# Even spacing of replicated loads, later GpSimd products and re-paced side DMAs in a selective-scan kernel

## Chip, cores and metric

The kernel runs on one core of a Trainium2 chip. The metric is the device time of one execution in microseconds; the median of several runs is given.

## What is computed

The reference is a network of four layers on four images of 64x64 positions and 96 channels. Nearly all of what follows concerns the selective scan of layer 0, cut here to what matters:

```python
x_hw = xc.reshape(B, D_INNER, L)                  # rows first; D_INNER = 192, L = 4096
x_wh = transpose(xc, (0, 1, 3, 2)).reshape(B, D_INNER, L)   # columns first
xs = concatenate([x_hw, x_wh, flip(x_hw), flip(x_wh)])
# per direction, image, channel d and state s (16 states):
#   h[t] = exp(delta[d, t] * A[d, s]) * h[t-1] + delta[d, t] * u[d, t] * B[s, t]
#   y[d, t] = sum over s of h[t] * C[s, t]
yy = y_rows + y_columns_turned_back + the two reversed ones
x = x + (yy * silu(z)) @ W_out.T
```

After it come, for each image, a depthwise and pointwise convolution (layer 1), a linear attention with a quantised feed-forward (layer 2), and a Fourier filter with another quantised feed-forward (layer 3). All data are float32.

## The kernel before

**Stages.** First the inputs of the scan of image 0 are made (projection, 3x3 convolution, softplus, products). Then comes the scan stage, an order written out by hand, and beside it run two lanes of other work. The drain and `tail()` handle what is left, above all layers 1 to 3 of image 3.

**Scan steps.** A half is one image in one order: `o = 0` is rows, `o = 1` is columns. `halves` (L1296) lists the eight of them. A half has 24 groups of 8 channels, so that 8 channels x 16 states fill 128 partitions; a group is a step, and `phases` lists all 192. A step covers the 4096 positions in four chunks of 1024. The loop at L1511 issues a step in eight slots, named f0 to f3 here (forward, `q` = 0 to 3) and b0 to b3 (backward, `k` = 0 to 3, chunk 3 - `k`).

In slot f`q`, VectorE scans chunk `q` forward from `pa` and `B` into `S` (L1534). In slot b`k` it scans backward into `pa` (L1581), saves the edge (L1587) and adds the two (L1588). Around it:

- ScalarE makes `pa` = exp(delta x A) in PSUM (`decay`, L1351), two buffers, seven times a step, one slot ahead.
- GpSimd multiplies delta·u by B (`times_b`, L1341) and the summed states by C (`times_c`, L1345), in place: `times_b(n + 1, q - 1)` in f1 to f3 and `times_b(n + 1, 3)` in b0 for the next step, `times_c` in b1 to b3 and in the next f0.
- TensorE sums over the states (`reduce`, L1361), ScalarE copies the sum (`result`, L1369), and SyncE stores it in four DMAs for each half of the positions (`store_result`, L1378).
- SyncE loads `dl` (`load_delta`) and `B` (`load_du`), four chunks each a step, every one replicated over 16 states in two DMAs (L1313). Tile `dl` has five buffers, `B` eight, `S` five. `load_rep` (L1336) fetches B and C of a new half into `rep0` and `rep1`, four chunks each.

SyncE issues all DMAs of the kernel in program order. Its DMAs take turns on eight completion semaphores, and a DMA waits until the one eight places before it has landed. Below, dl1 means `load_delta` of chunk 1, du3 `load_du` of chunk 3.

**Side lanes.** After each slot `pieces` (L1427) adds credit to five resources (TensorE, ScalarE, GpSimd, VectorE, DMA) from that slot's row of `gains` (L1419) and lets generators go on as far as their costs fit. The side lane transposes the scan inputs of an image for the columns (`turns`), turns the columns' result back (`turn_back`) and gates and projects it (`post`). These copies run on ScalarE (L166), with stores at L133 and `sz` products on VectorE at L514. A `turn` store takes 1.6 of DMA credit. The main lane first makes the scan inputs of images 1 to 3 (ScalarE `u`, L392; GpSimd, L469 to L477) and then works through layers 1 to 3 of images 0 to 2 (`rest`; feed-forward matmuls L967 and L987, ScalarE rows L958 to L996). `post` of an image waits for `done["scans", b]`, and `turn_back` for `done["columns", b]`. Which side operation falls into which slot is thus decided when the program is built.

Of the kernel before, what the change touches and what calls it, by code (L numbers as in the profile page):

```python
# [18 lines left out]
NB = 4  # L19
# [52 lines left out]
def layers(ctx: ExitStack, tc: tile.TileContext, a: dict, out):  # L72
# [101 lines left out]
    def halves_of(src, dst):  # L174
        return [(src[k * C : (k + 1) * C, :], dst[k * C : (k + 1) * C, :]) for k in range(2)]

    def turns(side, b):

        yield from until(lambda: done.get(("back", b), 0) == NBLK)
        pairs = [(bc_s[0][b], bc_s[1][b])]  # L180
        for s in (delta_s, du_s):
            pairs += halves_of(s[0][b], s[1][b])
        yield from turn(side, pairs)
        done["turns", b] = True

    def turn_back(side, b):

        yield from until(lambda: ("columns", b) in done)
        yield from turn(side, halves_of(y_s[1][b], y2_s[b]))
# [45 lines left out]
    def until(ready):  # L235
        while not ready():
            yield NEXT
# [1021 lines left out]
    def side_lane(take, side):  # L1259


        def place(name, k):
            at = 8 if name == "xr" else 2 * ("y_in", "u_in", "y2_in", "sz_in").index(name) + k % 2
            return side[:, at * BLK : (at + 1) * BLK]

        steps = [turns(side, 0), turns(side, 1), turn_back(side, 0), post(place, take, 0, 1)]
        steps += [turns(side, 2), turns(side, 3), turn_back(side, 1), post(place, take, 1, 1)]
        steps += [turn_back(side, 2), post(place, take, 2, 1), turn_back(side, 3)]
        for s in steps:
            yield [s], []  # L1270
# [22 lines left out]
        return slice(q * CH, (q + 1) * CH)  # L1293


    halves = [(b, o) for b in range(NB) for o in ((0, 1) if b < NB - 1 else (1, 0))]  # L1296
    phases = [(b, g, o) for b, o in halves for g in range(NG)]
    N = len(phases)
    dls, Bs, Ss, reps, pys, yss = {}, {}, {}, {}, {}, {}
# [1 line left out]
    def place_of(n, q):  # L1301


        return (4, 3, 2, 1)[q] if n % 2 else q
# [5 lines left out]
    def load_channels(t, src, g, q):  # L1310
        for k, part in enumerate(channel_halves(t)):
            rows = src[g * 8 + k * 4 : g * 8 + k * 4 + 4, chunk(q)]
            nc.sync.dma_start(part, rows.unsqueeze(0).broadcast_to([NS, 4, CH]))  # L1313

    def load_delta(n, q):
        if n < N:
            b, g, o = phases[n]
            t = dls[n, q] = big.tile([128, CH], F32, tag=f"dl{place_of(n, q)}", name="dl")
            load_channels(t, delta_s[o][b], g, q)
# [18 lines left out]
    def times_b(n, q):  # L1338

        if n < N:  # L1340
            nc.gpsimd.tensor_tensor(Bs[n, q], Bs[n, q], reps[n // NG, 0, q], ALU.mult)  # L1341

    def times_c(n, q):
        if n >= 0:
            nc.gpsimd.tensor_tensor(Ss[n, q], Ss[n, q], reps[n // NG, 1, q], ALU.mult)  # L1345
# [8 lines left out]
    def reduce(n, half):  # L1354

        if n < 0:
            return
        py = pys[n, half] = ps.tile([128, BLK], F32, tag="py", name="py")
        for j in range(4):
            q, k = 2 * half + j // 2, j % 2  # L1360
            nc.tensor.matmul(  # L1361
                py[32 * j : 32 * j + 32, :], lhsT=red, rhs=Ss[n, q][:, k * BLK : (k + 1) * BLK],
                start=True, stop=True,
            )

    def result(n, half):
        if n >= 0:
            ys = yss[n, half] = big.tile([128, BLK], F32, tag="ys", name="ys", bufs=2)
            nc.scalar.copy(ys, pys.pop((n, half)))  # L1369

    def store_result(n, half):
        if n < 0:
            return
        b, g, o = phases[n]
        ys = yss.pop((n, half))
        for j in range(4):
            i = 4 * half + j
            nc.sync.dma_start(  # L1378
                y_s[o][b][g * 8 : g * 8 + 8, i * BLK : (i + 1) * BLK], ys[32 * j : 32 * j + 8, :]
            )  # L1380
# [3 lines left out]
    class Lane:  # L1384
# [32 lines left out]
    credit = [0.0] * 5  # L1417

    gains = [  # L1419
# [4 lines left out]
    ]  # L1424
    cap = (4.4, 3.0, 3.2, 1.6, 4.0)

# [58 lines left out]
    take, _ = bank_taker(head.psum("head_psum"), 8)  # L1485
# [7 lines left out]
    take, banks = bank_taker(beside.psum("beside_psum"), 3)  # L1493
    ps = scan_psum.psum("scan_psum")
    side = big.tile([C, 9 * BLK + BLK // 2], F32, tag="side", name="side")
    lanes += [Lane(side_lane(take, side)), Lane(main_lane(take))]
    for q in range(NCH):
        load_rep(0, 0, q)
        load_du(0, q)
        load_delta(0, q)  # L1500
        times_b(0, q)
    for q in range(NCH):
        load_rep(0, 1, q)
    for q in range(3):
        load_du(1, q)
    load_delta(1, 0)

    with tc.manual_schedule():
        ordered[0] = True
        pa = decay(0, 0)  # L1510
        for n in range(N + 1):  # L1511
            h = n // NG
            end = n == N

            for q in range(NCH):
                if q == 0:
                    load_du(n + 1, 3)
                if q == 3:
                    load_delta(n + 1, 1)
                if n % NG == 0 and 0 < n < N and q > 0:  # L1520
                    load_rep(h, 1, 4 - q)
                later = decay(n, q + 1) if q < 3 else decay(n, 2)
                if q == 0:
                    times_c(n - 1, 0)
                else:
                    times_b(n + 1, q - 1)
                if q == 1:
                    reduce(n - 1, 0)
                if end:
                    if q == 0:  # L1530
                        result(n - 1, 1)
                    continue
                s = Ss[n, q] = big.tile([128, CH], F32, tag=f"S{place_of(n, q)}", name="S")
                nc.vector.tensor_tensor_scan(  # L1534
                    s, pa, Bs[n, q], Ss[n, q - 1][:, CH - 1 : CH] if q else 0.0, ALU.mult, ALU.add
                )
                if q < 3:
                    pa = later
                pieces(q)
                if q == 0:  # L1540
                    result(n - 1, 1)
            if end:
                result(n - 1, 0)
                store_result(n - 1, 1)
                store_result(n - 1, 0)
                break
            if n % NG == 0 and n > 0:
                load_rep(h, 1, 0)
            if n % NG == 1 and n > 1:
                b, o = halves[h - 1]  # L1550
                if o == 1:
                    done["columns", b] = True
                if o == 1 and b < NB - 1:
                    done["scans", b] = True

            for k, q in enumerate(reversed(range(NCH))):
                if k == 0:
                    times_b(n + 1, 3)
                    result(n - 1, 0)
                else:  # L1560
                    times_c(n, q + 1)
                if k == 1:
                    store_result(n - 1, 1)
                    store_result(n - 1, 0)
                    load_delta(n + 1, 2)
                if k == 2:
                    load_delta(n + 1, 3)
                if k == 3:
                    load_delta(n + 2, 0)
                if k > 0:  # L1570
                    load_du(n + 2, k - 1)
                if n % NG == NG - 2:
                    load_rep(h + 1, 0, k)
                if k == 1:
                    pa, later = later, decay(n, 1)
                elif k == 2:
                    pa, later = later, decay(n, 0)
                elif k == 3:
                    pa, later = later, decay(n + 1, 0)

                nc.vector.tensor_tensor_scan(  # L1581
                    pa[:, ::-1], pa[:, ::-1], Bs[n, q][:, ::-1],
                    edge if k else 0.0, ALU.mult, ALU.add,
                )
                if k < 3:
                    edge = big.tile([128, 1], F32, tag="edge", name="edge", bufs=2)
                    nc.vector.tensor_copy(edge, pa[:, 0:1])  # L1587
                nc.vector.tensor_tensor(Ss[n, q], Ss[n, q], pa, ALU.add)  # L1588
                if k == 3:
                    reduce(n, 1)  # L1590
                pieces(4 + k)
            pa = later
            if n % NG == NG - 4 and h + 1 < len(halves):
                b, o = halves[h + 1]
                assert done.get(("turns", b)) if o else done.get(("back", b)) == NBLK, (n, done)
# [119 lines left out]
```

## Time and profile before

Three runs took 6194.13, 6206.99 and 6194.72 us; the median is 6194.72. The profiled execution spans 6214.4 us.

| | us | share of the span |
|---|---|---|
| VectorE (DVE) busy | 4867.6 | 78% |
| TensorE (PE) busy | 4300.1 | 69% |
| GpSimd (POOL) busy | 4078.0 | 66% |
| ScalarE (ACT) busy | 3266.1 | 53% |
| DMA, q1 | 1167.71 MB | 69.3% of 16 engines |

The scan stage begins at 428 us, when the first scan starts, and ends at 5645 us. Measured from the first scan of one half to that of the next, its eight halves take 668.9, 638.7, 676.9, 649.4, 667.1, 627.5, 656.7 and 631.9 us.

Rows of the profile read as follows: a group gives line, engine, operation, output and inputs with their sizes and count, then busy time, mean ns of one, idle time before them and what ended it. A wait row gives who waited for whom, us in total, times and the longest. A row of the timeline gives start, duration, engine, line and operation, with the idle time before it in brackets. "SPq" is SyncE's queue.

### The profile page before, as it was taken

How to read it: one execution, taken by the hardware profiler on the slowest of the kernel's cores; microseconds unless marked ns; L12 is line 12 of the kernel's file. 1: busy time of each engine (PE TensorE's matmuls, PEld its weight loads, DVE VectorE, ACT ScalarE, POOL GpSimd, SP SyncE). 2: the span in 40 equal slices, each digit the busy share in tenths (PEclk: the TensorE clock that was granted, in tenths of full speed). 3: DMA queues.
4: the chain of work that ended last, by engine and by line, in shares of the span. 5: the costliest groups of instructions: out<-in, count | busy, mean ns of one | idle time of the engine just before them, and what ended most of it. 6: DMA issues, size and time to landing. Idle time of an engine off the chain costs nothing. (4 is left out here: it accounts for less than half of the span.)

```text
span 6214.4 us, 64018 instructions
## 1 busy us (share of the span) xinstructions
PE 4300.1 (69%) x19506; PEld 1860.1 (30%) x19506; DVE 4867.6 (78%) x3493; ACT 3266.1 (53%) x4443; POOL 4078.0 (66%) x1960
## 2 busy tenths in 40 slices
PE   6948888889884665563656765666446756668888
PEld 2312222223221121252411210544011204552386
DVE  2018888898989888998899899999998899994222
ACT  3536676677665356655464355444733474444513
POOL 0237888798988667776678678776876687763000
PEclk9968888878886775566757765677566756777887
DMA  3148777887788878788878766688888677884021
GB/s 82 45 111 222 225 209 213 232 234 212 202 234 236 212 193 215 195 230 235 237 211 226 205 176 179 181 231 217 222 221 215 160 211 199 220 221 132 8 72 62
DMA packets 468081, 1171.80 MB, mean 189 GB/s; under 512 B 90502, under 2 KB 155736, under 8 KB 467544
## 3 DMA queue, kind: packets, MB, share of 16 engines
q1 hardware_dynamic: 467736, 1167.71, 69.3%
q8 instruction: 154, 2.52, 0.2%
q14 instruction: 191, 1.56, 0.1%
HBM read 1012.17 MB, written 155.19 MB: 188 GB/s over the span
## 5 line engine op out<-in xcount | busy, mean ns | idle before, releaser
L1345 POOL TENSOR_TENSOR S<-S,rep 128x1024 f32<-128x1024 f32 x768 | 1808.8, 2359 | 738.0 <-DVE S L1588 680.2
L1351 ACT ACTIVATE pa<-dl,nega 128x1024 f32<-128x1024 f32 x1344 | 1498.6, 1117 | 1462.5 <-DVE S L1588 1098.3
L1341 POOL TENSOR_TENSOR B<-B,rep 128x1024 f32<-128x1024 f32 x768 | 1797.9, 2363 | 403.1 <-DMA B<-du_s 216.8
L1534 DVE TENSOR_TENSOR_SCAN S<-pa,S,B 128x1024 f32<-128x1024 f32 x576 | 1352.4, 2348 | 330.7 <-ACT pa L1351 151.9
L1581 DVE TENSOR_TENSOR_SCAN pa<-pa,edge,B 128x1024 f32<-128x1024 f32 x576 | 1354.3, 2351 | 62.7 <-ACT pa L1351 61.9
L1361 PE MATMUL py<-S,red 128*32 128x512 f32 x3072 | 633.3, 882 | 862.6 <-POOL S L1345 746.1
L379 PE MATMUL p_conv<-xp,conv_w 96*96 96x504 f32 (+3 forms) x2304 | 1066.4, 617 | 16.8 <-ACT r L450 7.7
L1588 DVE TENSOR_TENSOR S<-S,pa 128x1024 f32<-128x1024 f32 x768 | 931.8, 1213 | 6.6
L1534 DVE TENSOR_TENSOR_SCAN S<-pa,B 128x1024 f32<-128x1024 f32 x192 | 438.2, 2282 | 222.4 <-DMA B<-du_s 208.4
L379 PEld LDWEIGHTS p_conv<-xp,conv_w 96*96 96x96 f32 x2304 | 386.3, 171 | 683.5 <-issue 632.3
L1361 PEld LDWEIGHTS py<-S,red 128*32 128x32 f32 x3072 | 76.8, 128 | 1232.1 <-POOL S L1345 1012.9
L1581 DVE TENSOR_TENSOR_SCAN pa<-pa,B 128x1024 f32<-128x1024 f32 x192 | 440.7, 2295 | 5.0
L166 ACT COPY side<-side 96x256 f32<-96x256 f32 (+1 forms) x448 | 280.7, 627 | 162.0 <-DMA duT_s<-side 59.5
L471 POOL TENSOR_TENSOR r<-r,lg 96x512 f32<-96x512 f32 x64 | 81.2, 1269 | 327.0 <-ACT lg L456 327.0
L801 PE MATMUL p_mean<-t,centre 96*96 96x512 f32 x256 | 203.7, 914 | 110.7 <-ACT sq L793 49.7
L760 PE MATMUL p_l<-x,taps 96*96 96x504 f32 (+3 forms) x576 | 273.9, 632 | 6.9 <-DMA x<-x 6.9
L1058 PE MATMUL p_dft<-dft,hb 128*64 128x64 f32 x3072 | 231.2, 319 | 55.5 <-DVE hb L1021 55.5
L1037 PE MATMUL p_h<-w1s,ln 97*64 97x64 f32 x3072 | 232.2, 338 | 31.2 <-DVE ln L839 17.7
L1058 PEld LDWEIGHTS p_dft<-dft,hb 128*64 128x64 f32 x3072 | 227.2, 251 | 75.0 <-DVE hb L1021 52.7
L1037 PEld LDWEIGHTS p_h<-w1s,ln 97*64 97x64 f32 x3072 | 227.2, 251 | 70.7 <-issue 28.3
L539 PE MATMUL p_y<-side,ident 96*96 96x512 f32 x288 | 202.7, 859 | 59.9 <-DMA side<-y_s 55.3
L1369 ACT COPY ys<-py 128x512 f32<-128x512 f32 x384 | 221.8, 578 | 19.3 <-PE py L1361 16.8
(194 smaller groups left out, 5068.1 us busy)
## 6 DMA issues: line engine op xcount, KB each, us to landing
B<-du_s SPq DMA_DIRECT2D x768, 256.0 KB
dl<-delta_s SPq DMA_DIRECT2D x768, 256.0 KB
B<-duT_s SPq DMA_DIRECT2D x768, 256.0 KB
dl<-deltaT_s SPq DMA_DIRECT2D x768, 256.0 KB
z_s<-z SPq DMA_DIRECT2D x48, 512.0 KB
zl<-z_s SPq DMA_DIRECT2D x64, 384.0 KB
side<-y_s SPq DMA_DIRECT2D x96, 192.0 KB
rep<-bc_s SPq DMA_DIRECT2D x64, 256.0 KB
```

The costliest lines, as they stand in the source:

```text
L166: nc.scalar.copy(o.rearrange("p (w h) -> p w h", h=HW), t[:n, :].rearrange("p (h w) -> p w h", w=HW)[:, q * w : (q + 1) * w, :],)
L379: nc.tensor.matmul(pr[:, ra:rb, ca_:cb_], lhsT=conv_w[:, kc, ky * 3 + kx, oc * C : (oc + 1) * C], rhs=xp[:, kc, at + ra : at + rb, ca_ + d ...
L760: nc.tensor.matmul(p3[:, ra:rb, ca_:cb_], lhsT=taps[:, ky * 3 + kx, :], rhs=x[:, at + ra : at + rb, ca_ + dx : cb_ + dx], start=(k == 0), ...
L1037: nc.tensor.matmul(p[at : at + N1, j, :], lhsT=ln3[:, :, 8 * k + j], rhs=w1s[:, hs], start=True, stop=True,)
L1058: nc.tensor.matmul(p[ri * N1 : (ri + 1) * N1, j, :], lhsT=hb[:, :, 8 * k + j], rhs=dft1[:, ri, :], start=True, stop=True,)
L1341: nc.gpsimd.tensor_tensor(Bs[n, q], Bs[n, q], reps[n // NG, 0, q], ALU.mult)
L1345: nc.gpsimd.tensor_tensor(Ss[n, q], Ss[n, q], reps[n // NG, 1, q], ALU.mult)
L1351: nc.scalar.activation(pa, dls[n, q], AF.Exp, scale=nega[:, g : g + 1])
L1361: nc.tensor.matmul(py[32 * j : 32 * j + 32, :], lhsT=red, rhs=Ss[n, q][:, k * BLK : (k + 1) * BLK], start=True, stop=True,)
L1534: nc.vector.tensor_tensor_scan(s, pa, Bs[n, q], Ss[n, q - 1][:, CH - 1 : CH] if q else 0.0, ALU.mult, ALU.add)
L1581: nc.vector.tensor_tensor_scan(pa[:, ::-1], pa[:, ::-1], Bs[n, q][:, ::-1], edge if k else 0.0, ALU.mult, ALU.add,)
L1588: nc.vector.tensor_tensor(Ss[n, q], Ss[n, q], pa, ALU.add)
```

## The change

The replicated loads move to other slots: dl0 from b3 of the step before (`load_delta(n + 2, 0)`) to f2, dl2 from b1 to b0, du3 from f0 to f1. `times_b` moves one slot on: chunk 3 is multiplied in f1 of its own step, the others in f2, f3 and b0 of the step before. The y store of the second half of the positions moves from b1 to f2 of the same step. The fifth column of `gains`, DMA credit, is set anew. Images 1 and 2 now scan columns before rows, as image 3 did already; the marks that tell `post` and `turn_back` of it follow, and `turn_back` of image 1 is put ahead of `turns` of image 3.

```diff
-        steps += [turns(side, 2), turns(side, 3), turn_back(side, 1), post(place, take, 1, 1)]
+        steps += [turns(side, 2), turn_back(side, 1), turns(side, 3), post(place, take, 1, 1)]
...
-    halves = [(b, o) for b in range(NB) for o in ((0, 1) if b < NB - 1 else (1, 0))]
+    halves = [(b, o) for b in range(NB) for o in ((1, 0) if b else (0, 1))]
...
-        (2.6, 0.7, 0, 0.8, 0.9), (1.4, 1.2, 0, 0.8, 0.9),
-        (2.6, 1.2, 0, 0.8, 0.9), (2.6, 1.2, 0, 0.8, 0.9),
-        (3.8, 2.8, 1.2, 1, 1.4), (3.8, 2.4, 1.2, 1, 1.4),
-        (3.8, 2.4, 1.2, 1, 1.4), (2.6, 2.4, 1.2, 1, 1.4),
+        (2.6, 0.7, 0, 0.8, 1.8), (1.4, 1.2, 0, 0.8, 0.8),
+        (2.6, 1.2, 0, 0.8, 0.8), (2.6, 1.2, 0, 0.8, 0.8),
+        (3.8, 2.8, 1.2, 1, 1.6), (3.8, 2.4, 1.2, 1, 1.4),
+        (3.8, 2.4, 1.2, 1, 1.0), (2.6, 2.4, 1.2, 1, 1.6),
...
         load_delta(0, q)
-        times_b(0, q)
+        if q < 3:
+            times_b(0, q)
...
-    load_delta(1, 0)
...
-                if q == 0:
+                if q == 1:
                     load_du(n + 1, 3)
-                if q == 3:
-                    load_delta(n + 1, 1)
+                if q > 1:
+                    load_delta(n + 1, q - 2)
...
                 if q == 0:
                     times_c(n - 1, 0)
+                elif q == 1:
+                    times_b(n, 3)
                 else:
-                    times_b(n + 1, q - 1)
+                    times_b(n + 1, q - 2)
...
+                if q == 2:
+                    store_result(n - 1, 1)
...
-                if o == 1 and b < NB - 1:
+                if h % 2 == 0 and b < NB - 1:
                     done["scans", b] = True
...
                 if k == 0:
-                    times_b(n + 1, 3)
+                    times_b(n + 1, 2)
                     result(n - 1, 0)
+                    load_delta(n + 1, 2)
...
                 if k == 1:
-                    store_result(n - 1, 1)
                     store_result(n - 1, 0)
-                    load_delta(n + 1, 2)
                 if k == 2:
                     load_delta(n + 1, 3)
-                if k == 3:
-                    load_delta(n + 2, 0)
                 if k > 0:
                     load_du(n + 2, k - 1)
```

More of the change, by code (lines that the diff above doesn't have):

```diff
@@ L1562, in layers @@
                 if k == 1:
-                    store_result(n - 1, 1)
                     store_result(n - 1, 0)
-                    load_delta(n + 1, 2)
                 if k == 2:
                     load_delta(n + 1, 3)
-                if k == 3:
-                    load_delta(n + 2, 0)
                 if k > 0:
```

## The prediction

> **What bounds the kernel now.** The row of stretches comes first. The 192 scan steps run from 428 to 5645 us; the tail follows.
>
> ```profile
> core 0: us, PE busy (x) PEld busy (x) DVE busy (x) ACT busy (x) POOL busy (x), PEclk, DMA share, GB/s
> 428.00:5645.00 5217.00, 3479.80 (x15333) 1431.52 (x15334) 4693.92 (x3189) 2881.80 (x3826) 3969.00 (x1866) 0.70 0.79 212
> 5645.00:5727.00 82.00, 77.96 (x186) 27.77 (x184) 21.23 (x32) 36.80 (x65) 25.72 (x19) 0.86 0.63 183
> ```
>
> VectorE is busy 4694 of the 5217 us, 90%; no other engine is above 76%, and the DMA engines stand at 79%. The groups of the page say with what:
>
> ```profile
> L1534 DVE TENSOR_TENSOR_SCAN S<-pa,S,B 128x1024 f32<-128x1024 f32 x576 | 1352.4, 2348 | 330.7 <-ACT pa L1351 151.9
> L1581 DVE TENSOR_TENSOR_SCAN pa<-pa,edge,B 128x1024 f32<-128x1024 f32 x576 | 1354.3, 2351 | 62.7 <-ACT pa L1351 61.9
> L1588 DVE TENSOR_TENSOR S<-S,pa 128x1024 f32<-128x1024 f32 x768 | 931.8, 1213 | 6.6
> ```
>
> Eight scans of 2.3 us, four adds of 1.2 us and three small copies make a step; the shortest steps of the trace take 24.4 us from start to start, and 192 of these are 4685 us. The change touches none of this work. What it can win is the rest, 532 us, and of that only waiting: side work that VectorE itself does stays. The waits of VectorE inside the stage (470 to 5645 us; us in total, times, longest):
>
> ```profile
> DVE S L1534 <- ACT pa L1351: 151.0, 90, 9.2
> DVE pa L1581 <- ACT pa L1351: 61.9, 43, 18.3
> DVE side L514 <- DMA side<-sz_s: 37.8, 20, 5.7
> ```
>
> Most name ScalarE, which is busy only 55% of the stage. So I followed every wait over 0.3 us ahead of a scan one link further, to what had held the ScalarE instruction. There are 322 us of them (the very first scan left out): 69 us end at a late load of dl or B, 107 us at a DMA of the side lanes (mostly a store that had to land before ScalarE could reuse its buffer), 93 us at ScalarE held behind side matmuls, 24 us at the py matmuls, 25 us at ScalarE or GpSimd themselves, 4 us at others. With the 38 us of the sz row, 214 us of VectorE's waiting are late DMAs. One step shows how; first SyncE's queue, then ScalarE, then VectorE:
>
> ```profile
> 1137.30 7.92 SPq L1378 DMA_DIRECT2D yT_s<-ys  x8
> 1145.26 1.16 SPq L1313 DMA_DIRECT2D dl<-deltaT_s  x2
> ...
> 1154.15 0.53 SPq L133 DMA_DIRECT2D deltaT_s<-side  x1
> ```
>
> ```profile
> 1161.18 0.63 ACT L166 COPY side<-side 96x256 f32<-96x256 f32 x1 [8.47 <-DMA deltaT_s<-side]
> ```
>
> ```profile
> 1165.33 2.35 DVE L1534 TENSOR_TENSOR_SCAN S<-pa,S,B 128x1024 f32<-128x1024 f32 x1 [9.18 <-ACT pa L1351]
> ```
>
> Eight small y stores hold SyncE for 7.9 us, six replicated loads follow back to back, the side store gets out after them at 1154, and the scan starts 9.2 us late.
>
> **What the skill says.** The Trainium skill, "DMA: Bandwidth & Descriptors", section on the anatomy of one DMA, says that DMA engines wait for no semaphore: the issuing sequencer waits before it dispatches. The trace agrees: SyncE waits 436 us in the stage for ScalarE ahead of loads, and what stands behind waits too. The same page, section "Issuing engines are not separate DMA queues", says that all DMAs run on the same 16 engines and interleave; that is why side stores pay for bunched loads. Its fit, about 2 us plus bytes over 436 GB/s, would make a 256 KB load 2.6 us, an estimate; where GpSimd waited for a B load, the trace has 7.6 us from issue to landing on average (147 cases), so most of it is queueing, and the measurement decides. Its rules say to issue early and wait late, which is what the moves change.
>
> **The change part by part.** I write f0 to f3 for the four forward slots of a step (about 2.4 us each) and b0 to b3 for the backward ones (3.6 us each).
>
> *Loads.* Before, a step has du3 in f0, dl1 in f3, then eight y stores, dl2 and du0 in b1, dl3 and du1 in b2, dl0 and du2 in b3: six of eight loads in three slots, 10.8 us. Six loads are 3 MB; at the 212 GB/s of the stage that is 14.8 us, more than the slots have. After: du3 in f1, dl0 in f2, dl1 in f3, dl2 in b0, du0 in b1, dl3 and du1 in b2, du2 in b3, and the y stores are four in f2 and four in b1. The count and bytes stay (16 DMAs of 256 KB, 8 of 16 KB). SyncE needs 16 x 0.57 + 8 x 0.30 = 11.5 us of issue a step either way, so issue is no bound. The time left from issue to use, by slots: dl2 goes from four slots, b1 to f1, less the stores ahead of it, to five; dl0 from eight to five, about 15.6 us, still twice 7.6; dl1 and dl3 stay.
>
> *GpSimd's B products a step later.* du0, du1, du2 get five slots to land instead of four, du3 eight instead of four. GpSimd waits 193 + 154 us for B in the stage; I expect nearly all of that gone, worth little in itself since VectorE waits only 11 us for these products. The price: B3 of a step is now made in f1, two slots ahead of its scan in f3. It follows the C product of f0, so it is ready 2 x 2.36 us after that one begins. Replayed on the trace of before, the margin at f3 is positive in all 191 steps, smallest 0.67 us, and in the built order a side operation (1.27 us) stands between the two in only 14 of 191. Cost 0, at most 5 us.
>
> *A new wait.* The load of the next half's rep for q = 3 stands in b3 of the last but one step of a half, but its buffer is now read in f1 of the last step. In the built program this DMA waits for that product. SyncE so stands from about the start of b3 to 5 us into the next step, some 7 us, seven times. Behind it stand side stores; the next replicated load, du3 in f1, has eight slots. Cost between 0 and 7 x 5 = 35 us; I take 5.
>
> *Credits.* DMA credit per step goes from 9.2 to 9.8 and moves to slots with few loads (f0 from 0.9 to 1.8, b2 from 1.4 to 1.0). It paces side work and makes none.
>
> *Order of halves.* Images 1 and 2 do columns first, so turning their columns back happens beside their rows, and their post starts when the image is done. By the built order the post of image 2 ends at step 155 instead of 161, and all side work is done by step 191; before, 22 of the 70 ffn blocks that ScalarE handles after the last decay are image 2's. Those lie in the drain now, 5645 to 5727 us, where the chain of waits puts p_f L967 at 6.0%, p_f L987 at 5.7%, the y rows of ScalarE at 5.8%, p_rstd at 2.3%: 17 us of 85. I take -17 (0 to -30: the post has its own loads). The work moves into the stage: 6 layer norm rows of VectorE at 0.67 us, 4 us, and some 60 rows of ScalarE, 37 us, at the ratio of waiting now (93 us behind side matmuls on 2882 busy, of which 1500 is decay, 6.7%) 3 us; I take +9 in all.
>
> *Sum.* Of 214 us of late DMAs I take half away, 107: the direct ones (69) mostly, since their spare time grows by 2.4 to 7 us against waits of mostly 1 to 4 us, less 13 us at the start that stay; the side lanes' 107 + 38 by a third to a half, since they have other causes too. The share is the unknown: from 0.2 (43) to 0.9 (193). -107 - 17 + 9 + 5 = -110 us on the profiled span of 6214.4, so 6104. That execution is 0.3% above the median of 6194.7 (three runs, 6194.1 to 6207.0); from the median it would be 6085. Since the terms lean on one another I take -100 from the median: **6095**.
>
> **The rivals.** *Little:* the lanes run ahead until something else stops them, and ScalarE then stands behind side matmuls (93 us now, TensorE's clock at 0.70). Then only the direct loads (about 45) and the tail (17) count, less 14: 6145 to 6175, say 6150. For it: in halves 5 to 8 side DMAs hold VectorE only 8 us. Against: 80 of the 107 us lie in the first two halves.
> *More:* all 214 us and the tail go, and the py and GpSimd waits with them: about 6000. Against: DMA share stays 79%.
> *Slower:* the y stores of the second half move from b1 to f2, two slots after ScalarE's copy that feeds them instead of five. SyncE waits 128 us for these copies now, 56 times, longest 10.4, while in the backward half; in f2 the wait stands ahead of dl1, dl2 and the side stores, where VectorE has only 2.4 us a slot. It decides once the wait passes some 3 us for a side store ScalarE needs; if two thirds of 128 reach VectorE (+85) and the lanes gain nothing, less the tail: 6195 + 85 - 17 = 6263. Against: with two slots between, ScalarE waits only 13 us for py ahead of these copies.
> *Not what it says:* the rep wait and the shorter lead of dl0 undo the even spacing: about no change, 6190.
>
> **How the numbers follow.** Forecast 0.57 (6045 to 6150), little 0.17, more 0.08, slower 0.13, not what it says 0.05. The measurement can tell about 0.2%, 12 us, from no change. Faster: 0.57 + 0.16 + 0.08 = 0.81; same 0.05; slower 0.14. The range 6025 to 6190 leaves out the slower case and the far end of "more".
>
> **What would show it.** Right: B waits of GpSimd fall from 347 us below 100; ACT side and ACT u waits for stores fall by a third; no run of eight L1378 issues; the stage shrinks by some 90 us and the drain by some 15, with no p_f in it. Wrong: the stage as long as now with ACT pa waits turned to PE releasers (little), or SyncE's wait for ys above 200 us (slower), or waits of S L1534 for POOL B above 30 us.

## The result and the profile after

The changed kernel takes 6094.0 us (median of 4 runs, 6087.3 to 6110.6) against 6194.4 before; the ratio is 0.984 (95% interval 0.9814 to 0.9865). The profiled execution spans 6085.3 us against 6214.4. Of these 129 us, 110 come off the scan stage (5107 against 5217 us), 14.5 off what follows it (555 against 569.4), and 5 off the start, whose code hardly changed. The medians are only 100 us apart: the profiled execution of before was 20 us above its median, that of after 7 us below, so differences between the two profiles hold some scatter.

The stretches of the changed kernel, the scan stage and the drain after it (columns as before):

```profile
core 0: us, PE busy (x) PEld busy (x) DVE busy (x) ACT busy (x) POOL busy (x), PEclk, DMA share, GB/s
423.00:5530.00 5107.00, 3436.51 (x15387) 1417.70 (x15388) 4695.17 (x3195) 2918.78 (x3882) 3987.85 (x1882) 0.71 0.80 217
5530.00:5600.00 70.00, 63.19 (x132) 21.38 (x130) 16.69 (x25) 5.62 (x9) 5.99 (x4) 0.84 0.70 199
```

VectorE does the same 4695 us of work in a stage that is 110 us shorter: its idle time fell from 523 to 412 us. Nothing became faster; less is waited for. ScalarE's 5.6 us in the drain are what is left of the 36.8 us there, since image 2's last feed-forward is gone from it. The chain of waits through the drain (5530 to 5605 us) holds no p_f row any more:

```profile
by line: PE p_y L539 54.0%; PE p_out L566 18.7%; DMA xr<-in_xT 5.3%; DMA x<-x 4.7%; PE p_l L760 4.7%; POOL S L1346 3.1%; DVE xr L571 2.8%; PE py L1362 2.6%; ACT xr L575 1.7%; DVE S L1590 1.6%; DVE sz_in L514 0.8%; SPq L133 0.8%; issue 0.7%;
```

The waits of VectorE in the stage (470 to 5540 us), the same three rows as before:

```profile
DVE S L1540 <- ACT pa L1352: 69.3, 53, 5.7
DVE pa L1583 <- ACT pa L1352: 59.8, 38, 5.6
...
DVE side L514 <- DMA side<-sz_s: 14.3, 9, 3.6
```

The forward scans' wait for ScalarE fell from 151 to 69 us, its longest from 9.2 to 5.7; the backward scans' hardly moved (62 to 60); the sz row fell from 38 to 14. What GpSimd waited for ahead of its B products, over the whole execution:

```profile
  DMA B<-duT_s: 53.5, 19
  DMA B<-du_s: 39.9, 11
```

Before, these were 154 and 217 us; inside the stage the sum fell from 347 to 60. Followed back one link as in the prediction, the 322 us of waits ahead of scans are now 244: late dl and B 38 us (69 before), side DMAs 83 (107), side matmuls ahead of ScalarE 81 (93), the rest 43 (53). In the 83 are 18 us of waits of forward scans that the profile ends at y stores; no scan reads what a y store writes, so what really ended these is not known.

### The profile page after: what moved, and what is told of

Read it like the earlier page. It is cut to its first block, busy times and chain, and to the rows that moved or that the text cites. A ratio compares the mean times of both kernels' runs of the same rounds, so it can differ in the third digit from the quotient of the medians.

```text
span 6085.3 us, 64390 instructions
## 1 busy us (share of the span) xinstructions
PE 4238.8 (70%) x19506; PEld 1838.9 (30%) x19506; DVE 4864.5 (80%) x3492; ACT 3271.8 (54%) x4443; POOL 4077.2 (67%) x1961
## 5 line engine op out<-in xcount | busy, mean ns | idle before, releaser
L1362 PE MATMUL py<-S,red 128*32 128x512 f32 x3072 | 617.9, 870 | 811.3 <-POOL S L1346 738.4
L379 PE MATMUL p_conv<-xp,conv_w 96*96 96x504 f32 (+3 forms) x2304 | 1050.0, 610 | 15.3 <-ACT u L392 12.4
L967 PE MATMUL p_f<-q,w_L 96*128 96x512 fp8e5 x192 | 100.2, 554 | 167.6 <-ACT y L958 87.0
```

Of the source, the lines that this page charges most:

```text
L379: nc.tensor.matmul(pr[:, ra:rb, ca_:cb_], lhsT=conv_w[:, kc, ky * 3 + kx, oc * C : (oc + 1) * C], rhs=xp[:, kc, at + ra : at + rb, ca_ + d ...
L1362: nc.tensor.matmul(py[32 * j : 32 * j + 32, :], lhsT=red, rhs=Ss[n, q][:, k * BLK : (k + 1) * BLK], start=True, stop=True,)
```

## Experiments

All but the first row were timed in five rounds beside the kernel before, in three groups (e1 to e4, e5 to e8, e9 to e12), whose medians for it were 6197.5, 6196.8 and 6197.3 us. Kernels of different groups are compared by their medians here; differences of some 10 us between them are not settled. "Old credits" are the kernel before's fifth column of `gains`.

| kernel | median us | ratio to before (95%) |
|---|---|---|
| changed kernel | 6094.0 | 0.984 (0.9814 to 0.9865) |
| e1 moves only | 6089.1 | 0.9815 (0.9796 to 0.9833) |
| e2 order of halves only | 6173.9 | 0.9954 (0.9938 to 0.9969) |
| e3 credits only | 6221.6 | 1.0035 (1.0026 to 1.0045) |
| e4 changed, old credits | 6077.0 | 0.9794 (0.9776 to 0.9812) |
| e5 e4, products back | 6071.8 | 0.9802 (0.9786 to 0.9819) |
| e6 e4, eight stores in b1 | 6153.8 | 0.9932 (0.9914 to 0.9951) |
| e7 e4, dl loads back | 6079.6 | 0.9812 (0.9796 to 0.9827) |
| e8 e4, rep load later | 6065.3 | 0.979 (0.9772 to 0.9808) |
| e9 before, store split and order | 6108.3 | 0.9859 (0.9839 to 0.9879) |
| e10 e4, eight stores in f2 | 6147.8 | 0.9922 (0.9904 to 0.994) |
| e11 e8, stores in four runs of two | 6049.2 | 0.9765 (0.9749 to 0.9782) |
| e12 changed, f0 credit 1.2 | 6103.7 | 0.9851 (0.9834 to 0.9867) |

### Which of the three parts

**e1: loads, stores and products moved; credits and order as before.** (The other rows of `gains`, the `turns` list and the `done` mark go back as well.)

```diff
 the changed kernel, with
...
-    halves = [(b, o) for b in range(NB) for o in ((1, 0) if b else (0, 1))]
+    halves = [(b, o) for b in range(NB) for o in ((0, 1) if b < NB - 1 else (1, 0))]
...
-        (2.6, 0.7, 0, 0.8, 1.8), (1.4, 1.2, 0, 0.8, 0.8),
+        (2.6, 0.7, 0, 0.8, 0.9), (1.4, 1.2, 0, 0.8, 0.9),
...
```

> The changed kernel with the old DMA credits and the old order of halves: only the loads, y stores and B products are moved. If the spacing of the replicated loads makes the gain (my theory), 6195 falls to about 6115 and GpSimd's wait for B falls from 347 to under 100 us, as in the changed kernel. If the credits make it (rival), at most 20 us come off: 6175 or more. If the order of halves makes it: 6180 or more.

6089, 108 us off, 26 more than expected: the moves alone make all of the gain. The 5 us by which this beats the changed kernel are within the intervals. VectorE's waits that end at a side DMA fell from 107 to 34 us, further than in the changed kernel (83).

**e2: order of halves alone.**

```diff
 the kernel before, with
+        steps += [turns(side, 2), turn_back(side, 1), turns(side, 3), post(place, take, 1, 1)]
...
+    halves = [(b, o) for b in range(NB) for o in ((1, 0) if b else (0, 1))]
...
+                if h % 2 == 0 and b < NB - 1:
                     done["scans", b] = True
```

> The kernel before with columns of images 1 and 2 first and nothing else. My theory: the work of image 2 leaves the drain, worth 10 to 20 us: about 6180, with the scan stage as long as before. A rival in which the order makes most of the gain: below 6140.

6174, 24 us off, somewhat over the 10 to 20. In its profile what follows the stage is 9 us shorter; the rest seems to lie inside the stage, which I had expected to stay as long, but of the stage's 25 us in the profiles some are scatter.

**e3: the new credits alone, and e4: the changed kernel with the old ones.** The edit is the fifth column of `gains`, put in or put back.

> The kernel before with the new DMA credits alone. With the loads still bunched in b1 to b3, more side DMAs in f0 should neither help nor hurt much: 6185 to 6200 by my theory. If pacing of side DMAs is the cause: 6150 or less.

> The changed kernel with the old DMA credits. My theory: spacing and order stay, 6100 to 6115. If the credits matter only together with the new spacing: 6140 or more.

Alone they cost 24 us, and taking them out of the changed kernel gains 17: 6077, a better version. I had expected neither help nor harm alone, and a loss on taking them out. Where they cost shows in ScalarE's waits in the first two halves (470 to 1736 us). The changed kernel, then e4:

```profile
ACT sz L361 <- PE p_z L355: 59.6, 16, 10.0
```

```profile
ACT sz L361 <- PE p_z L355: 26.8, 17, 3.8
```

In these halves the copies of `p_z` wait 20 to 32 us in all eleven kernels with the old column, but 68, 60 and 51 in e3, the changed kernel and e12, which have the new one or most of it; and the backward scans' wait for ScalarE is 15 to 40 us in the eleven, 67, 43 and 58 in the three. My reading is that the credits shift the side DMAs of the projection, and with them the slot in which ScalarE meets a matmul that is not done; the rows show the wait, not that cause.

**e12: the new credits with f0 at 1.2.**

```diff
-        (2.6, 0.7, 0, 0.8, 1.8), (1.4, 1.2, 0, 0.8, 0.8),
+        (2.6, 0.7, 0, 0.8, 1.2), (1.4, 1.2, 0, 0.8, 0.8),
```

> The changed kernel with f0's DMA credit at 1.2 instead of 1.8, so that a step has 9.2 as before. The new credits cost 17 us (6094 against 6077). If their amount, or the burst in f0, is the cause: 6070 to 6082. If the distribution over the other slots is: 6088 to 6100.

6104: it does not come back. So neither the sum of the credits nor the size of the burst in f0 is the cause; what is left is how the column falls on the slots. Which slot it is was not tried.

### Which of the moves

e5 to e7 undo one move each in e4 (6077); e8 to e11 try other places.

**e5: products and du3 back.**

```diff
-                if q == 1:
+                if q == 0:
                     load_du(n + 1, 3)
...
-                elif q == 1:
-                    times_b(n, 3)
                 else:
-                    times_b(n + 1, q - 2)
+                    times_b(n + 1, q - 1)
...
                 if k == 0:
-                    times_b(n + 1, 2)
+                    times_b(n + 1, 3)
```

> The changed kernel with the old DMA credits (6077), and the B products and du3 back in their old slots; dl loads and y stores stay moved. My theory: the products' later slots are worth little, since VectorE waits only 11 us for them: 6080 to 6095, while GpSimd's waits for B come back to above 200 us. Rival, that GpSimd's waiting for B was what held the steps: 6130 or more.

6072: the products' later slots gain nothing. And GpSimd's waits for B did not come back: 75 us in the stage against 35 in e4. So it was not the later slot that cured most of these waits.

**e6: eight y stores in b1 again.**

```diff
-                if q == 2:
-                    store_result(n - 1, 1)
...
                 if k == 1:
+                    store_result(n - 1, 1)
                     store_result(n - 1, 0)
```

> The changed kernel with the old DMA credits, and all eight y stores in b1 again; loads and products stay moved. If the run of eight stores ahead of dl2, du0 and the side stores was the main cause (the step shown at 1137 us): 6120 or more. If the spacing of the loads is: 6080 to 6100.

6154: of e4's 120 us, 77 are gone. VectorE's waits in the stage, e4 first:

```profile
DVE S L1540 <- ACT pa L1352: 83.3, 60, 6.4
DVE pa L1583 <- ACT pa L1352: 42.7, 35, 5.1
...
DVE side L514 <- DMA side<-sz_s: 9.6, 5, 3.2
```

```profile
DVE S L1538 <- ACT pa L1352: 132.0, 75, 10.0
DVE pa L1583 <- ACT pa L1352: 42.4, 43, 6.7
...
DVE side L514 <- DMA side<-sz_s: 34.6, 12, 5.1
```

The forward scans' wait and the sz row are most of the way back to the kernel before (151 and 38 us); the backward scans' wait (62 there) does not move. Followed back as above, the waits ahead of scans are 283 us in e6 against 233 in e4: late dl and B and side DMAs have some 30 us more each, side matmuls some 13 less.

**e7: dl0 back in b3 of the step before, dl2 back in b1.**

```diff
-                if q > 1:
-                    load_delta(n + 1, q - 2)
+                if q == 3:
+                    load_delta(n + 1, 1)
...
                     result(n - 1, 0)
-                    load_delta(n + 1, 2)
...
                 if k == 1:
                     store_result(n - 1, 0)
+                    load_delta(n + 1, 2)
...
+                if k == 3:
+                    load_delta(n + 2, 0)
```

> The changed kernel with the old DMA credits, and dl0 back in b3 of the step before, dl2 back in b1; products, du3 and y stores stay moved. If six loads in b1 to b3 were the main cause: 6125 or more, with the side lanes' DMA share of the waits back above 70 us. If not: 6080 to 6100.

6080, no loss that can be measured, with six loads in b1 to b3 as before. The waits at side DMAs did rise from 68 to 85 us, as the prediction's theory of six loads had it, but those behind side matmuls fell from 82 to 51.

**e10: all eight stores together in f2.**

```diff
                 if q == 2:
+                    store_result(n - 2, 0)
                     store_result(n - 1, 1)
...
                 if k == 1:
-                    store_result(n - 1, 0)
```

> The changed kernel with the old DMA credits, and all eight y stores together in f2, where few loads stand (the first half of the positions a step later). If a run of eight stores is harmful wherever it stands: 6130 or more. If only its place ahead of dl and du in the backward half is: 6065 to 6090.

6148, as if a run of eight hurt where few loads stand just as in b1. But its trace shows a second cause. There are two `ys` tiles, and the first half of the sums now stays in one until f2 of the next step. ScalarE's waits in the stage:

```profile
ACT ys L1370 <- DMA yT_s<-ys: 227.8, 41, 13.3
ACT ys L1370 <- DMA y_s<-ys: 111.9, 30, 10.3
```

In e6 these are 3 us, in e4 none. All of them are of the copy in b0, which needs the tile that the first four stores of the run empty; whenever one ended, at most these four had been issued, so the four behind them were not its cause. Followed back as above, the scans wait 295 us in e10 against 233 in e4; of the 62 us more, 43 end, by way of ScalarE, at y stores and 10 at late dl and B. So e10 loses its time mostly by the late place of the first half's stores, and does not separate the run from the place.

**e9: the split of the stores and the order of halves, on the kernel before.** (The lines for the order are those of e2.)

```diff
+                if q == 2:
+                    store_result(n - 1, 1)
...
                 if k == 1:
-                    store_result(n - 1, 1)
                     store_result(n - 1, 0)
```

> The kernel before with two parts of the change alone: the y store of the second half in f2, and the order of halves; loads, products and credits as before. If the split of the stores is what the spacing part owes its gain to: 6075 to 6100. If it needs the moved loads or products as well, each of which could be undone alone without loss: 6120 or more.

6108, between the two expectations. Against e2, the order alone, this split is worth 66 us. The moved loads and products are worth the other 31 us to e4, though each could be undone alone at no cost; I take it that with either in place the loads have room enough, which was not tried further. With the old slots for all of them, e9's GpSimd still waits for B, though less than e2's (187 and 108 us):

```profile
POOL B L1341 <- DMA B<-duT_s: 132.2, 52, 9.0
POOL B L1341 <- DMA B<-du_s: 39.6, 26, 4.5
```

**Why a run of eight.** A DMA waits until the one eight places before it has landed; in the trace every one of SyncE's 6245 DMAs carries the semaphore of the one eight places before. When the last of eight stores of 16 KB is issued, all loads ahead of the run have therefore landed, nothing large is in flight, and the DMA engines run dry. The stretches of the kernel before, 2 us before and 2 us after the run of eight stores shown in the prediction (its last issue ends at 1145.2; the last three columns are clock, DMA share and GB/s):

```profile
1135.30:1137.30 2.00, 0.00 (x0) 0.00 (x0) 1.97 (x4) 1.97 (x3) 1.52 (x1) 1.00 1.05 308
1145.20:1147.20 2.00, 0.00 (x0) 0.00 (x0) 1.97 (x2) 1.84 (x3) 2.00 (x3) 0.50 0.33 64
```

The same in the changed kernel, about a step of the same half. Its queue first, then 2 us before and after the first run of four, before and after the second:

```profile
1170.55 1.16 SPq L1314 DMA_DIRECT2D dl<-deltaT_s  x2
1171.81 2.33 SPq L1379 DMA_DIRECT2D yT_s<-ys  x4
1174.47 2.16 SPq L1314 DMA_DIRECT2D dl<-deltaT_s  x2
...
1179.85 1.28 SPq L1379 DMA_DIRECT2D yT_s<-ys  x4
1182.64 1.45 SPq L1314 DMA_DIRECT2D B<-duT_s  x2
```

```profile
1169.80:1171.80 2.00, 2.00 (x6) 0.20 (x8) 1.81 (x2) 1.97 (x4) 2.00 (x2) 0.50 1.01 255
1174.10:1176.10 2.00, 0.32 (x1) 0.24 (x2) 2.00 (x1) 2.00 (x5) 2.00 (x2) 1.00 1.00 178
1177.80:1179.80 2.00, 2.00 (x4) 0.67 (x3) 1.97 (x4) 0.00 (x0) 1.25 (x2) 0.54 1.00 281
1181.10:1183.10 2.00, 2.00 (x6) 0.68 (x5) 1.97 (x3) 0.00 (x0) 2.00 (x2) 1.00 0.97 197
```

From 308 to 64 GB/s across eight stores, with the DMA engines a third busy; across the two runs of four of this step they stay full (255 to 178 GB/s, and 281 to 197). Over all runs of stores in the stage, a packet counted where it ends, the median rate in the 2 us after the run is 59 GB/s in the kernel before, 48 in e6 and 57 in e10, all with runs of eight; 218 in the changed kernel and 210 in e4 with runs of four; 240 in e11 with runs of two. Counted where a packet starts, as in the stretches, they are 87, 80, 73, 206, 201 and 231. The rate after a run is not all there is to it: e7 and e9, also with runs of four but with the dl loads in their old slots, have 152 and 121 GB/s, and e7 takes no longer than e4. SyncE's time in one run has a median of 4.9, 4.8 and 5.2 us with eight, 1.4 with four and 0.8 with two.

So it is shown that the engines run dry after eight stores in a row, in b1 and in f2 alike, and that putting four of them elsewhere is worth 66 us (e9 against e2) to 77 (e4 against e6). That the dry stretch, and not the mere place of the four stores ahead of du0, costs these us is my reading: no run has eight stores in b1 with loads between them.

**e8: the rep load after its last reader.**

```diff
-                if n % NG == NG - 2:
+                if n % NG == NG - 2 and k < 3:
                     load_rep(h + 1, 0, k)
+                if n % NG == NG - 1 and k == 0:
+                    load_rep(h + 1, 0, 3)
```

> The changed kernel with the old DMA credits, and the load of the next half's rep for chunk 3 issued in b0 of the last step of a half, after its buffer's last product, so that SyncE has nothing to wait for there. I priced that wait at 5 us (0 to 35): 6065 to 6077. If it costs nothing, 6077.

SyncE's wait is gone. e4 first, then e8:

```profile
SPq L1337 <- POOL B L1342: 46.1, 10, 9.6
```

```profile
SPq L1337 <- POOL B L1342: 2.3, 4, 1.0
```

The median falls 12 us, but the ratios (0.979 and 0.9794) hardly differ, so whether this gains anything is not settled.

**e11: stores two by two, on e8.**

```diff
-                if q == 2:
-                    store_result(n - 1, 1)
+                if q > 1:
+                    store_result(n - 1, 1, (2 * q - 4, 2 * q - 3))
...
-                if k == 1:
-                    store_result(n - 1, 0)
+                if k in (1, 2):
+                    store_result(n - 1, 0, (2 * k - 2, 2 * k - 1))
```

> The changed kernel with the old DMA credits, the rep load in b0 of the last step, and the y stores two each in f2, f3, b1 and b2. If shorter runs of stores go on helping: 6055 or less, against 6065 without. If two runs of four are short enough: 6060 to 6070.

6049 (6047.5 to 6054.7), another 16 us below e8 (6055.5 to 6076.4), and the best version here: 148 us below the kernel before. The intervals of the two ratios just touch, and half of the stores have also moved to f3 and b2, so that shorter runs are the cause is not shown by this alone. The waits of VectorE in its stage:

```profile
DVE S L1540 <- ACT pa L1352: 63.3, 55, 3.9
DVE S L1540 <- PE py L1362: 34.2, 19, 3.8
DVE S L1540 <- DVE S L1540: 33.0, 131, 0.3
DVE pa L1585 <- ACT pa L1352: 29.9, 29, 3.8
```

Against the changed kernel the backward scans' wait has halved (60 to 30; 35 in e8), and in these rows none is longer than 3.9 us.

## Why the prediction was right, and where it was not

- *Late DMAs, -107 of 214 us.* Right in kind, and near in size: the moves alone gave 108 (e1). VectorE's waits at dl, B, side DMAs and sz fell from 214 us (69, 107, 38) to 135 in the changed kernel (38, 83, 14), 79 less, and to about 102 in e1. ScalarE's waits for side stores, which I wanted to see fall by a third, fell from 192 us to 77.
- *Which move does it.* Here the reasoning failed. I laid the gain on six loads in three slots, "more than the slots have": 14.8 us at the stage's 212 GB/s against 10.8. But 212 is the mean with the dry stretches in it, at a DMA share of 0.79. From 1147 to 1153 us, at a share of 1.00, the engines moved 278 GB/s, at which the six loads take 11.3 us, about what the slots have. And I counted the y stores at 8 x 0.30 us of issue. That term was mis-sized: a run of eight takes SyncE 4.9 us in the median, and behind it the engines have little in flight. The run was in the step I showed, and I read it as a queue that was held up (one side store, at 1150 us, did get out among the six loads); I did not see that the DMA engines went idle meanwhile. Of e4's 120 us, undoing the split takes 77 back; undoing the dl loads, 3.
- *Products a step later, about 0.* Right in time (e5). The fall of GpSimd's B waits came as forecast, 347 to 60 us in the stage, but most of it not from the later slots: e5 has 75 without them, and the split of the stores alone took some 120 (e9 against e2).
- *The rep wait, +5.* SyncE waits 37 us in all there in the changed kernel, longest 11.4. By e8 its cost is between nothing and some 12 us, inside the bounds of 0 and 35; the 5 can't be told from that.
- *Order and drain, -17 + 9.* The part after the stage shrank by 14.5 us in the changed kernel, but by 8 to 12 in e2, e4, e8 and e11, which have the new order and the old credits. The order alone gave 24 in all, so the +9 in the stage did not come; why the stage too seems shorter in e2 stays open.
- *Credits, 0.* Wrong: +17 in the changed kernel, +24 alone. The working said that credit "paces side work and makes none"; but with the new pacing ScalarE waits twice as long for `p_z`.
- *The sum.* That the forecast of 6095 lies this close to 6094 is luck, since terms missed in opposite ways: moves and order gave 120 us where the sum had 110 and I took 100, and the credits took 17 back.
- *The rivals.* "Slower" needed SyncE's wait for ys above 200 us; it went from 128 to 154. "Little" needed VectorE's waits to turn to side matmuls; that row fell, 93 to 81. "More" was added up wrongly: late DMAs and tail gone, less the 14 us for rep and the moved work, make 5978, and less with the py and GpSimd waits, not 6000.

## What to carry to other kernels

Where one queue carries large loads and small stores with a fixed number in flight, look for places where as many small ones follow each other as may be in flight, and try breaking the run, two or four at a time, between large transfers; here that was worth 66 to 77 us. Read the DMA rate in the microseconds after such a run, not its mean over the stage, which was 212 GB/s before and 217 after. When a change bundles moves, undo each alone and also do the suspected one alone; two moves here were free to undo singly and worth 31 us together. And when an undoing moves something to a new place, see in its trace whether it waits for something else there, as e10 does for its `ys` tiles.

## What was not expected of the hardware

Eight stores of 16 KB in a row, 0.29 us of issue each in the median, brought the DMA rate from 205 to 59 GB/s (medians of the 2 us before and after the run, a packet counted where it ends), and below 100 GB/s after every one of the 190 runs. In e6 and e4, which differ in the place of four of the stores alone, it is 48 and 210 GB/s after the run.
